# Layer 3 window attention: sums of neighbouring widest states on GpSimd, and one product per stretch of query columns

## The chip, the cores and the metric

The kernel runs on one core of a Trainium2 chip. One launch computes four layers one after the other on an input of 4 images, 256 channels, 48 by 48 pixels, in float32. The metric is the device time of the launch in microseconds (us), as the median of several runs; smaller is better. Five engines work side by side[...]: TensorE (PE in the profile, its weight loads PEld), VectorE (DVE), ScalarE (ACT), GpSimd (POOL) and SyncE (SP), on whose queue nearly all transfers are issued.

## The reference, cut to what matters

Layers 0 to 2 are convolutions and aren't touched. Layer 3 is a windowed linear attention with 8 heads of d = 32 channels, over square windows of 48, 24 and 12 pixels around each pixel:

```python
q = jax.nn.sigmoid(q); k = jax.nn.sigmoid(k)
v = v / jnp.maximum(jnp.linalg.norm(v, axis=1, keepdims=True), 1e-12)
...
for w in WINDOWS:                       # 1, 2, 4
    ws = Hh // w                        # 48, 24, 12
    wk = _box(Ik, ws, Hh, Ww)           # sum of k over the window
    wkv = _box(Ikv, ws, Hh, Ww)         # sum of the 32x32 matrices k v^T over the window
    attn = jnp.einsum('bdhw,bdfhw->bfhw', q, wkv)
    norm = jnp.einsum('bdhw,bdhw->bhw', q, wk)
    attn = attn / (norm[:, None] + 1e-06)
    outs.append(attn.reshape(b, C, Hh, Ww))
```

The three results are concatenated, multiplied by Wout and added to the layer's input. For a pixel, `attn` is the sum over all keys of its window of (q . k) v. It can be computed key by key (scores q . k, masked, times v), or, for a whole tile of keys that a query sees entirely, as q times the tile's state, the 32x32 matrix sum of k v^T.

## The kernel before, in words

**Tiling.** The image is cut into 6 row blocks of 8 rows (`RB`, `NRB`). A key tile is 8 rows by 16 columns, 128 keys (`KC`, and 3 of them side by side, `NKC`). A block of work is one image, one half of the heads (4 heads on 128 partitions) and one row block of queries (384 columns): 4 x 2 x 6 = 48 blocks, in the list `order` (line 2276).

**Steps.** Each block goes through a list of steps (`steps_of`, line 1968). A step computes the scores of some key tiles into PSUM (`scores`, tile `s`), lets ScalarE and VectorE mask them into SBUF (`masked`, tile `sm`; GpSimd masks the smallest window out of the middle one's), and two steps later (`LAG`) multiplies them with the values (`sums`, tiles `acc0` to `acc2`, one per window). The PSUM room for scores is that of one step (`ps_s`, two tiles), so a step's scores can start only when the step before is masked. `whole` (line 2120) is called in step 4 (`WHOLE`) of each block. For the widest window (48, half width 24) it adds what needs no scores: for the key tiles that a query sees entirely, the query times the state. A key tile of column number c is seen entirely by the query columns `cols_whole(c)` (line 100): columns 0 to 24 for c = 0, 8 to 40 for c = 1, 24 to 48 for c = 2. For each of the three c, and each of the four heads, there is one product: 32x32 weights, and 192, 256 or 192 columns (8 rows for each column). A float32 product is two MATMUL instructions in the trace, so a block has 24 of them, all named `acc<-qs,kv`. The four heads lie on four different partition quarters in and out.

**The states.** `window_state(i)` (line 1879) adds on GpSimd the states of the row blocks that are entirely within reach, into the tile `kv` (3 x 32 numbers in each partition): one `tensor_add` for the first two, one for each further row block. It is started at step 3 of the block before (`midway`, line 2316).

**The order of work.** Each engine executes in the order in which this program emits. Beside the steps, jobs written as generators are emitted in between: projections of the next image (`Projection`), the states (`state`), the norms (`norms`, `inverse`), their prefix sums (`k_sums`), and the ends of blocks (`prepare`, `finish`, whose products are `out_ps`). `advance(time, pool_time)` (line 347) is called once a step. `time` is an estimate of what TensorE has to spare in that step (line 2397: 1200 ns + the time of the masks - the time of the sums, where `sums_time`, line 2356, includes `whole`), and goes into a budget, `spare`, that a job's products must find filled (`turn`, `bank`). GpSimd has such a budget too (`slack`): `pool_turn` (line 377) charges `190 + 1.95 * elements` ns for each operation, and an urgent one is charged without waiting.

All instructions go through one helper, so that the profile has line 251 for all; they are told apart by their tiles.

Of the kernel before, what the change touches and what calls it, by code (L numbers as in the profile page):

```python
# [12 lines left out]
F32 = mybir.dt.float32  # L13
# [9 lines left out]
P = 128  # L23
B, C, H, W = 4, 256, 48, 48
# [3 lines left out]
RB = 8  # L28
# [47 lines left out]
HEADS, D = 8, 32  # L76
# [4 lines left out]
NKC = W // KC  # L81
# [18 lines left out]
def cols_whole(c):  # L100

    return max(0, c * KC + KC - HALVES[0]), min(W, c * KC + HALVES[0])


MID = W // 2
# [15 lines left out]
def strips(half):  # L121

    got = []
    for c, x0, x1 in PARTS[half]:
        f0, f1 = cols_whole(c)
        got.append((c, x0, f0) if x0 < f0 else (c, f1, x1))
    return got
# [127 lines left out]
def conv_preact_kernel(  # L255
# [53 lines left out]
    pe, dve, act, pool, sync = (  # L309
        InOrder(tc, e) for e in (nc.tensor, nc.vector, nc.scalar, nc.gpsimd, nc.sync)  # L310
    )
# [57 lines left out]
    def wait_for(*keys):  # L369
        while not made.issuperset(keys):  # L370
            yield 1

    def pool_op(elements):

        return 190 + 1.95 * elements

    def pool_turn(elements, times=1, urgent=False):

        nonlocal slack
        cost = times * pool_op(elements)  # L380
        while slack < 0.5 * cost and not urgent:
            yield 1
        slack -= cost
# [21 lines left out]
    def product_time(columns):  # L405

        return 1.67 * columns
# [192 lines left out]
    with (  # L600
# [479 lines left out]
        def load_row(pool_, tag, a):  # L1080

            t = pool_.tile([P, NCT, K0, P], F32, tag=tag, name="wrow")
            sync.dma_start(
                out=t, in_=w1[:, a * K0 : (a + 1) * K0, :].rearrange("(ct p) k o -> p ct k o", p=P)
            )
            return t
# [442 lines left out]
        with tc.tile_pool(name="wst", bufs=1) as wst:  # L1529
            for ct in range(NCT):  # L1530
                fetch_x(0, ct)
            rows = [load_row(k1p, "k1", 0), load_row(vp, "v", MT), load_row(vp, "v", MT - 1)]
# [15 lines left out]
            for ct in range(NCT):  # L1548
                for k0, k1 in TAPS:
# [3 lines left out]
                    else:  # L1553
                        pool_, tag = {
                            (0, 0): (xp, "x1_0"),
                            (0, 2): (xp, "x1_1"),
                            (1, 0): (wst, "raw1"),
                            (1, 2): (wst, "raw"),
                        }[ct, k0]
# [70 lines left out]
    with (  # L1630
# [248 lines left out]
        def window_state(i):  # L1879


            b, ct, rb = order[i]
            rows = [a for a in range(NRB) if rows_whole(a, rb)]
            yield from wait_for(*(("state", b, ct, a) for a in rows))
            st = states[b, ct]
            yield from pool_turn(NKC * D, len(rows) - 1, urgent=True)
            t = scr.tile([P, NKC, D], F32, tag="kv", name="kv", bufs=2)
            pool.tensor_add(t, st[:, rows[0]], st[:, rows[1]])
            for a in rows[2:]:
                pool.tensor_add(t, t, st[:, a])  # L1890
            wides[i] = t
            made.add(("window", i))

# [16 lines left out]
        def rows_whole(a, rb):  # L1910

            return abs(a - rb) * RB + RB <= HALVES[0]
# [89 lines left out]
        class Block:  # L2002
# [117 lines left out]
            def whole(self, i):  # L2120

                t = wides.pop(i)
                for c in range(NKC):
                    c0, c1 = cols_whole(c)
                    for j in range(HG):
                        head = slice(j * D, (j + 1) * D)
                        pe.matmul(
                            self.accs[0][head].rearrange("p (w r) -> p w r", w=W)[:, c0:c1],
                            t[head, c, :],
                            self.qs[head, c0:c1],  # L2130
                            start=False,
                            stop=False,
                        )
# [182 lines left out]
        def midway(i):  # L2316

            b, ct, rb = order[i]
            if (b, ct) == (0, 0) and 0 < rb <= NRB - seen_first:
                a = seen_first - 1 + rb  # L2320
                until(("k", 0, 0, a), ("v", 0, a))
                load_kv(0, 0, a)
            if ct == NCT - 1:
                start(prepare(i))
            if i + 1 < len(order):
                start(window_state(i + 1), ahead=True)
                nb, nct, nrb = order[i + 1]
                until(("q", nb, nct, nrb))
                qs[i + 1] = load_q(*order[i + 1])
# [18 lines left out]
        def mask_time(st):  # L2348

            on_act = 150 + 0.87 * 2 * (st.hi - st.lo)  # L2350
            if not st.parts[1]:
                return on_act
            on_dve = sum((2 * part[-1] + 130) / 0.96 for part in st.parts[1])
            return 2 * max(on_act, on_dve)

        def sums_time(st, at):

            time = sum(product_time(part[-1]) for parts in st.parts for part in parts)
            if at == WHOLE:
                time += product_time(sum(RB * (c1 - c0) for c0, c1 in map(cols_whole, range(NKC))))  # L2360
            return time

        def far_time(st):
# [2 lines left out]

        blocks, ahead = {}, []
        start(window_state(0))
        start(finish_all())
        for n in range(len(stream) + LAG):  # L2370
            if n < len(stream):
                i, st, at, last = stream[n]
                if at == 0:
                    begun(i)
                ss = blocks[i].scores(st)
                ahead.append(blocks[i].masked(st, ss))
                if at == MIDWAY:
                    midway(i)
            if n >= LAG:
                i, st, at, last = stream[n - LAG]  # L2380
                sms = ahead.pop(0)
                if at == 0:
                    if i >= 2:
                        until(("done", i - 2))
                    blocks[i].begin()
                if at == WHOLE:
                    until(("window", i))
                    blocks[i].whole(i)
                for wi in (1, 0, 2):
                    if st.parts[wi]:  # L2390
                        blocks[i].sums(wi, st, sms)
                if last:
                    done(i)
            time, pool_time = 1000.0, 1000.0
            if LAG <= n < len(stream):
                pool_time = 3600.0 - far_time(stream[n][1])
                time = 1200.0 + mask_time(stream[n][1]) - sums_time(*stream[n - LAG][1:3])
            advance(max(time, 500.0), max(pool_time, 150.0))
# [46 lines left out]
```

## Time and profile before

| | |
|---|---|
| time, median of 3 runs | 3193.77 us (3187.84 to 3198.49) |
| profiled execution: time / span in the profile | 3194.66 us / 3192.8 us |
| PE busy | 2866.5 us, 90% of the span |
| PEld busy | 2024.3 us, 63% |
| DVE busy | 2002.8 us, 63% |
| POOL busy | 1356.8 us, 42% |
| ACT busy | 994.5 us, 31% |
| mean granted TensorE clock | 0.955 |
| first and last product `acc<-qs,kv` of Layer 3 | 1441.3 us, 3169.7 us |
| products `acc<-qs,kv` | 1152 MATMUL |
| additions into `kv` on POOL | 48 of two states, 96 of a further one |

Busy time is that of the whole span. A line of a table of groups names engine, operation and `out<-in` tiles. A window line gives the busy time of each engine within a stretch, with the number of instructions behind it, then the granted TensorE clock, the share in which the transfer engines were busy, and GB/s. A line of the timeline gives the start, the length, the engine and what was executed how many times in a row, and in brackets the idle time before it and what ended that. The chain lists, in order of time, the pieces of work each of which was released by the one before; it leads back from the last instruction, so work that isn't on it was hidden behind something.

### The profile page before, as it was taken

The numbers are of one execution on the slowest core, as the hardware profiler recorded it, in microseconds if no ns is written. First come the engines' busy times: TensorE is split into PE (matmuls) and PEld (weight loads), VectorE is DVE, ScalarE is ACT, GpSimd is POOL, SyncE is SP. The second block draws the span as 40 slices with busy tenths as digits, with TensorE's granted clock in tenths as the row PEclk, the third lists the DMA queues.
The fourth block names the chain that finished last, engine by engine and source line by source line (L and its number), as shares of the span: only waits on it lengthen the run. The fifth ranks groups of instructions, "written<-read, shape, count | busy, mean of one in ns | idle before, by whom it ended". The sixth has DMA issues, their size and how long they took to land.

```text
span 3192.8 us, 98649 instructions
## 1 busy us (share of the span) xinstructions
PE 2866.5 (90%) x42698; PEld 2024.3 (63%) x42698; DVE 2002.8 (63%) x3779; ACT 994.5 (31%) x1965; POOL 1356.8 (42%) x1915
## 2 busy tenths in 40 slices
PE   3678999898989987889998899898999989999999
PEld 2456868677766856576665556565666655666665
DVE  7976658747855831376776666675546765555454
ACT  0002211121111144325543235553236532333322
POOL 0000012003000312046788877787757687644443
PEclk9788899999999988899999999999999999999999
DMA  8746512431443144324565765564544456411222
GB/s 276 212 161 185 159 62 103 130 123 53 136 123 110 60 127 146 111 79 140 162 200 147 215 187 156 163 192 142 162 138 144 141 157 186 134 40 44 89 76 69
DMA packets 380037, 434.05 MB, mean 136 GB/s; under 512 B 129843, under 2 KB 335443, under 8 KB 378451
## 3 DMA queue, kind: packets, MB, share of 16 engines
q1 hardware_dynamic: 378403, 425.76, 43.3%
q8 instruction: 338, 5.54, 0.8%
q0 software_dynamic: 144, 1.17, 0.2%
q10 hardware_dynamic: 1056, 0.79, 0.1%
q14 instruction: 96, 0.79, 0.1%
HBM read 288.11 MB, written 140.68 MB: 134 GB/s over the span
## 4 chain that ended last, share of the span: by engine, by line
PE 62%; DVE 11%; POOL 4%; DMA 4%; ACT 3%; issue 2%; SPq 2%; ACTq 0%; DVEq 0%; POOLq 0%
PE s L251 16%; PE cv L251 15%; PE acc L251 15%; PE out_ps L251 5%; PE proj_ps L251 5%; PE ap L251 3%; DVE sm L251 2%; DVE l2v L251 2%; SPq L251 2%; POOL sm L251 2%; POOL nhi L251 1%; ACT sm L251 1%; DVE v L251 1%; PE keys_ps L251 1%; DVE x L251 1%
## 5 line engine op out<-in xcount | busy, mean ns | idle before, releaser
L251 DVE TENSOR_TENSOR sm<-s,masks 128x448 f32<-128x448 f32 (+9 forms) x1408 | 619.9, 497 | 437.1 <-PE s L251 379.5
L251 POOL TENSOR_TENSOR sm<-sm,masks 128x704 f32<-128x704 f32 (+11 forms) x512 | 596.5, 1186 | 513.9 <-DVE sm L251 513.5
L251 ACT ACTIVATE sm<-s 128x384 f32<-128x384 f32 (+2 forms) x736 | 441.5, 609 | 746.6 <-PE s L251 589.7
L251 PE MATMUL cv<-vx,wt 128*128 128x288 f32 x2080 | 562.6, 427 | 92.2 <-DVE vx L251 49.9
L251 PE MATMUL s<-qs,ks 32*128 32x320 f32 (+10 forms) x8704 | 589.1, 360 | 34.7 <-ACT sm L251 20.1
L251 PE MATMUL acc<-sm,vs 128*32 128x128 f32 (+19 forms) x18432 | 606.0, 276 | 6.3 <-issue 6.2
L251 PEld LDWEIGHTS acc<-sm,vs 128*32 128x32 f32 x18432 | 443.0, 110 | 190.2 <-issue 143.4
L251 PEld LDWEIGHTS s<-qs,ks 32*128 32x128 f32 x8704 | 395.1, 186 | 256.2 <-issue 112.0
L251 PEld LDWEIGHTS cv<-vx,wt 128*128 128x128 f32 x2080 | 404.5, 199 | 214.6 <-issue 56.8
L251 POOL MEMSET v<- 128x16 f32 (+1 forms) x120 | 18.7, 216 | 765.0 <-DVE vx L251 639.8
L251 PE MATMUL cv<-v,wl 128*128 128x384 f32 x1152 | 226.8, 357 | 27.3 <-DVE x L251 9.4
L251 PEld LDWEIGHTS cv<-v,wl 128*128 128x128 f32 x1152 | 216.7, 197 | 38.4 <-issue 17.9
L251 DVE TENSOR_SCALAR sm<-s 128x896 f32<-128x896 f32 (+1 forms) x96 | 110.9, 1156 | 116.0 <-PE s L251 92.5
L251 PE MATMUL s<-masks 24*128 24x192 bf16 (+3 forms) x1664 | 168.3, 284 | 0.0
L251 POOL TENSOR_TENSOR v<-l2v,v 128x384 fp32r<-128x384 f32 x96 | 108.5, 1160 | 120.4 <-ACT v L251 111.7
L251 PE MATMUL cv<-pad,wl 128*128 128x384 bf16 x864 | 145.5, 331 | 5.1 <-ACT pad L251 5.1
L251 POOL TENSOR_TENSOR nhi<-nhi,nq 128x384 f32<-128x384 f32 x144 | 147.9, 1047 | 0.0
L251 PE MATMUL out_ps<-o,wout_sb 128*32 128x384 f32 x1152 | 122.0, 495 | 6.2 <-ACT ns L251 2.4
L251 PEld LDWEIGHTS <-wl 128*128 128x128 bf16 x864 | 84.5, 98 | 65.5 <-issue 7.9
L251 PE MATMUL out_ps<-stage,wout_sb 128*32 128x384 f32 x1152 | 121.8, 491 | 0.2 <-issue 0.2
L251 DVE TENSOR_TENSOR pt<-cs 128x184 f32<-128x184 f32 x144 | 120.1, 838 | 0.1
L251 PE MATMUL ap<-seen,xT 120*128 120x120 f32 (+3 forms) x832 | 120.1, 304 | 0.0
(175 smaller groups left out, 3419.8 us busy)
## 6 DMA issues: line engine op xcount, KB each, us to landing
wt<-wt SPq DMA_DIRECT2D x48, 768.0 KB
kb_d<-pt SPq DMA_DIRECT2D x48, 576.0 KB
rc<-r_d SPq DMA_DIRECT2D x192, 144.0 KB
nhi<-kb_d SPq DMA_DIRECT2D x120, 192.0 KB
nlo<-kb_d SPq DMA_DIRECT2D x88, 192.0 KB
o_d<-stage SPq DMA_DIRECT2D x24, 576.0 KB
o<-o_d SPq DMA_DIRECT2D x24, 576.0 KB
wl<-wl_d SPq DMA_DIRECT2D x16, 768.0 KB
```

The source lines that it names most:

```text
L251: return lambda *args, **kwargs: self.tc.keep_in_program_order(op(*args, **kwargs))
```

## The change

The query columns are cut where the set of entirely seen key tiles changes: at 0, 8, 24, 40 and 48. Columns 0 to 8 see tile 0 alone, 8 to 24 tiles 0 and 1, 24 to 40 tiles 1 and 2, 40 to 48 tile 2 alone. GpSimd makes two more states for each block, 0 + 1 and 1 + 2, with one further `tensor_add` of 64 numbers in each partition, and `whole` then runs one product for each head and stretch: 64, 128, 128 and 64 columns. The tile `kv` grows from 3 x 32 to 5 x 32 numbers. The two estimates that the planner uses, of the cost on GpSimd and of the columns in `whole`, follow.

```diff
+def whole_ranges():
+
+    cuts = sorted({x for c in range(NKC) for x in cols_whole(c)})
+    got = []
+    for x0, x1 in zip(cuts, cuts[1:]):
+        cs = [c for c in range(NKC) if cols_whole(c)[0] <= x0 and x1 <= cols_whole(c)[1]]
+        got.append((x0, x1, cs))
+    return got
+
+
+WHOLES = whole_ranges()
...
-            yield from pool_turn(NKC * D, len(rows) - 1, urgent=True)
-            t = scr.tile([P, NKC, D], F32, tag="kv", name="kv", bufs=2)
-            pool.tensor_add(t, st[:, rows[0]], st[:, rows[1]])
+            yield from pool_turn(NKC * D, len(rows), urgent=True)
+            t = scr.tile([P, 2 * NKC - 1, D], F32, tag="kv", name="kv", bufs=2)
+            alone, pairs = t[:, 0:NKC], t[:, NKC:]
+            pool.tensor_add(alone, st[:, rows[0]], st[:, rows[1]])
             for a in rows[2:]:
-                pool.tensor_add(t, t, st[:, a])
+                pool.tensor_add(alone, alone, st[:, a])
+            pool.tensor_add(pairs, alone[:, 0 : NKC - 1], alone[:, 1:NKC])
...
-                for c in range(NKC):
-                    c0, c1 = cols_whole(c)
+                for x0, x1, cs in WHOLES:
                     for j in range(HG):
                         head = slice(j * D, (j + 1) * D)
                         pe.matmul(
-                            self.accs[0][head].rearrange("p (w r) -> p w r", w=W)[:, c0:c1],
-                            t[head, c, :],
-                            self.qs[head, c0:c1],
+                            self.accs[0][head].rearrange("p (w r) -> p w r", w=W)[:, x0:x1],
+                            t[head, cs[0] + (NKC if len(cs) == 2 else 0), :],
+                            self.qs[head, x0:x1],
...
-                time += product_time(sum(RB * (c1 - c0) for c0, c1 in map(cols_whole, range(NKC))))
+                time += product_time(sum(RB * (x1 - x0) for x0, x1, _ in WHOLES))
```

More of the change, by code (lines that the diff above doesn't have):

```diff
@@ L102, in cols_whole @@
     return max(0, c * KC + KC - HALVES[0]), min(W, c * KC + HALVES[0])
+def whole_ranges():
[6 more added lines that the diff above has]
+WHOLES = whole_ranges()
+assert all(cs in ([c] for c in range(NKC)) or cs in ([c, c + 1] for c in range(NKC - 1)) for _, _, cs in WHOLES)
 MID = W // 2
```

## The prediction

> **What bounds the kernel now.** I read the page's busy times first, then the windows by stage, the timeline around one widest product, the chain of waits in each 50 us of Layer 3, and the waits. Busy times of PE and POOL over the whole span, then four windows (length, then PE, PEld, DVE, ACT, POOL busy, clock, DMA share):
>
> ```profile
> PE 2866.5 (90%) x42698; PEld 2024.3 (63%) x42698; DVE 2002.8 (63%) x3779; ACT 994.5 (31%) x1965; POOL 1356.8 (42%) x1915
> ...
> 1693.00:1772.00 79.00, 58.94 (x1024) 33.76 (x1016) 44.63 (x80) 21.16 (x50) 70.39 (x91) 0.87 0.57 165
> 2012.00:2032.00 20.00, 11.82 (x328) 8.98 (x320) 10.76 (x21) 3.99 (x13) 15.14 (x27) 0.88 0.79 202
> 2032.00:2215.00 183.00, 180.62 (x4007) 117.85 (x4008) 137.18 (x242) 89.77 (x194) 151.84 (x224) 0.98 0.50 157
> 2690.00:3193.00 503.00, 478.91 (x10616) 320.94 (x10608) 258.38 (x511) 152.88 (x275) 235.52 (x248) 0.99 0.28 80
> ```
>
> The reader is to see that Layer 3 has two regimes. In most of it (2032 to 2215 stands for it) PE is busy 95 to 99%: time taken off PE there is time taken off the run. In short stretches around the norms of an image (1693 to 1772: PE 75%, POOL 89%) something else leads. The chain says what:
>
> ```profile
> 1734.52 2.51 POOL sm L251 x2
> 1737.03 1.43 POOL nhi L251
> 1738.46 2.50 POOL sm L251 x2
> 1740.96 1.43 POOL nhi L251
> ```
>
> There POOL works without a pause and PE waits for the norm's operands. Four stretches are led by POOL, the SP queue or a transfer: 1693-1772, 1861-1885, 2012-2032 and 2560-2690. (One at 2215-2230 has no widest product in it.)
>
> The widest product itself, in the timeline of one block:
>
> ```profile
> 2326.83 1.28 PE L251 MATMUL acc<-qs,kv 32*32 32x192 f32 x24
> 2328.05 0.66 PE L251 MATMUL acc<-sm,vs 128*32 128x156 f32 x16
> ```
>
> From its start to the next group's it takes 2328.05 - 2326.83 = 1.22 us. And a block in which the masks lead, not PE:
>
> ```profile
> 2864.66 2.40 DVE L251 TENSOR_TENSOR sm<-s,masks 128x312 f32<-128x312 f32 x8 [1.23 <-PE s L251]
> 2864.67 1.28 PE L251 MATMUL acc<-qs,kv 32*32 32x192 f32 x24
> 2865.89 1.05 PE L251 MATMUL acc<-sm,vs 128*32 128x112 f32 x32
> 2866.87 1.27 PE L251 MATMUL s<-qs,ks 32*128 32x320 f32 x13
> ```
>
> DVE reads the scores until 2867.06; the next scores begin at 2866.87 in the half already read and need the other half at once. A shorter widest product would only make PE wait here.
>
> **What the skill says.** (1) "TensorE: Matmul & The Clock Gate", Part 3, The mechanism: matmuls at different 32x32 tile positions run concurrently, their starts some 4 ns apart. The trace agrees: 24 instructions of 192 or 256 columns in 1.22 us are possible only with four heads at once. (2) The same page, Back-to-back issue gap: for 1 to 64 columns there is an issue floor of about 60 cycles, 25 ns. The 64-column stretches of the change lie at it, so it is my upper bound for them; the trace speaks against it as a price per instruction of a group of four (`kv_ps` below: 8 ns each). (3) "TensorEngine Tiling (Array Packing)", Key Properties: changing the tiling mode drains the engine. The mode changes into and out of the widest product remain, so that cost stays. (4) "GPSIMD Engine Reference", 3.1: a two-input float32 add costs about 2.6 cycles an element, over a fixed dispatch; the trace agrees (next part).
>
> **The change part by part.**
>
> *Products on PE.* Prices of four concurrent heads, one instruction each ("a quad"), come from the chain:
>
> ```profile
> 2302.44 0.19 PE kv_ps L251 x24
> ...
> 2319.24 0.66 PE keys_ps L251 x24
> ...
> 2331.65 1.29 PE out_ps L251 x16
> ```
>
> Six quads of 32 columns take 0.19 us, 32 ns each; six of 128 columns 0.66 us, 110 ns; four of 384 columns 1.29 us, 322 ns. From 128 columns up that is 0.84 to 0.86 ns a column. Before: four quads of 192 (161 ns) and two of 256 (215 ns) = 1.07 us, so that 0.15 of the 1.22 us is fixed. After: four quads of 128 = 0.44 us and four of 64. I take 56 ns for these (the same line, 0.86 to 0.88 ns a column): 0.22 us. Sum 0.66 + 0.15 = 0.81 us; 0.41 us saved in a block, 48 x 0.41 = 19.7 us. Bounds for the 64-column quad: not under 32 ns, since 32 columns take that; not over 4 x 25 = 100 ns, the page's issue floor paid four times (an estimate). That gives 0.51 to 0.23 us a block, 24 to 11 us in all. The 8 further weight loads are 32x32, 105 ns each and overlapped; 24 of a larger form pass within 0.19 us in `kv_ps`, so no cost.
>
> *The addition on POOL.* 128x64 isn't in the trace; its neighbours are:
>
> ```profile
> L251 POOL TENSOR_TENSOR kp<-kp,carry x5: 282/288/387, 1705.5 to 1770.3; 128x48 f32<-128x48 f32 x5
> ...
> L251 POOL TENSOR_TENSOR kv<-kv,state x96: 386/390/876, 1440.5 to 3126.9; 128x96 f32<-128x96 f32 x96
> ```
>
> 48 numbers take 288 ns, 96 take 390: 2.1 ns each, so 64 take 0.32 us (bounds 0.29 and 0.39). 48 x 0.32 = 15.4 us of POOL. Queued behind it are masks for the smallest window and norm work. Away from the stretches POOL idles for DVE (487.0 us in the list of waits), which hides it. The state is made a block ahead; PE waited for `kv` once in the run, 1.8 us, in the first block. There the addition lies bare: 0.3 us, about cancelled by the first group's running at a lower clock, where the saving is larger.
>
> *Saving that isn't kept.* Six widest products start in stretches led by others (1714.8, 1868.2, 2015.5, 2571.0, 2601.6, 2650.3): 6 x 0.41 = 2.5 us lost. Five of these are on POOL's side and pay the addition as well: 5 x 0.32 = 1.6 us. In two more the masks end with the product as in the timeline above (1789.7, 2899.0) and nothing covers: 0.7 us. Some eight have 0.36 to 0.40 us between masks and scores: 8 x 0.05 = 0.4 us. Together 5.2 us. In two others of that pattern (2191.3, and 2864.7, the one shown) the emitted order of the changed kernel has `out_ps` products (1.29 us) put into the step, which cover the wait; were they not, 0.8 us more would be lost.
>
> *What is moved.* The planner finds 0.43 us more to spare in step 4 of every block and charges GpSimd 0.38 us more. In the emitted order of the two kernels the projections come about one step earlier (888 of 1092 instructions), out products too, and the norms of the last image up to some six steps later. No instruction kind changes in number, but for 6 divisions that go straight from PSUM on DVE and save 6 copies on ACT. The transfers issued by SP are the same 1710, in slightly other places. Cost: nothing on average, for the sum of inserted PE work is the same; but which of the waits at the norms get longer or shorter isn't fixed, and single ones are 2.7 to 8.3 us long. I carry +-8 us for it.
>
> *Sum.* 3194.66 (the profiled execution, of which 1.9 lie outside the span) - 19.7 + 5.2 = 3180.2. That execution was 0.9 above the median of 3193.77, so 3179.3 for a median; I say 3180. What is late next is what is now: PE, and in the stretches POOL.
>
> **The rivals.**
>
> *A. The forecast*, a net gain of 7 to 22 us, 3180.
>
> *B. The waits at the norms shrink as well.* PE idles at the norms for about 20 + 8 + 9 + 13 us in the stretches. With norms emitted later against PE, some of the waits fall away. For: of the 144 norm products 39 move later and 12 earlier. Against: their POOL work moves with them. Full 19.7 and 6 us of waits: 3168.
>
> *C. The time doesn't go.* POOL's 15.4 us would lie on the path in most blocks, since POOL is 83% busy in 2032-2215, and PE would wait for masks in place of its own products. For: mask waits follow every block. Against: in that stretch PE is 99% busy, with POOL waiting for DVE. About 3191.
>
> *D. Slower: a store of V stuck behind norm loads on SP.*
>
> ```profile
> ACT vt L251 <- DMA v_d<-vt: 13.2, 2, 10.4
> ```
>
> At 2021-2031 ACT waits 10.4 us for the store of an earlier `vt`, which SP issues only after a row of norm loads; PE then idles 8.3 us in front of `proj_ps`. With projections a step earlier, more stores could fall into such rows. To be slower by 0.3% it needs 14 + 9.6 = 24 us, three more such stalls: 3180 + 25 = 3205. Against it: in the emitted order, stores of `vt` with ten or more norm loads among the 22 transfers before them are 6 before and 5 after.
>
> **How the numbers follow.** A 0.58, B 0.14, C 0.18, D 0.10. 0.3% is about what a measurement of this kernel can tell from no change: 9.6 us, so faster is under 3184.2, slower over 3203.4. Of A some 0.06 lies above 3184.2. Faster 0.52 + 0.14 = 0.66; within 0.06 + 0.18 = 0.24; slower 0.10. The range of 3166 to 3196 takes in A, most of B and two thirds of C, and with them both ends of the 64-column price (3175 to 3189).
>
> **What would show it.** In the profile after: the widest product at 0.8 us from start to next group (right), near 1.0 if the issue floor holds (PE's step wrong); `kv<-kv` 128x64 at 0.32 us; PE busy lower by some 20 us with its idle time in Layer 3 up by a few; POOL up by 15 us; waits of PE and PEld for POOL `nhi` within some us of their 64. The forecast is wrong if these waits, or that for `v_d<-vt`, grow by 10 us or more, or shrink so.

## The result, and the profile after

The change takes 3166.98 us (median of 8 runs, 3147.29 to 3175.78) against 3193.52 us before (8 runs beside it): a ratio of 0.9912, 95% interval 0.989 to 0.9933. By that ratio it is 28 us less (the two medians themselves lie 26.5 us apart; from here on, differences between run times are taken from the ratios). Two repeats on other occasions gave 0.9919 (0.9906 to 0.9931) and 0.9924 (0.9908 to 0.994), or 26 and 24 us. Forecast were 14.

The profiled execution took 3175.78 us, its span 3174.0. Busy times on its page:

```profile
PE 2852.3 (90%) x43082; PEld 2034.6 (64%) x43082; DVE 1989.3 (63%) x3779; ACT 991.4 (31%) x1959; POOL 1368.6 (43%) x1963
```

POOL has 48 more instructions and 11.8 us more work; PE is 14 us less busy. From the first widest product on, PE is busy 1661.7 us before and 1639.7 us in the change, which is 22 us less; the rest of the difference lies in Layers 0 to 2. One widest product in the timeline of the change, the counterpart of the one at 2326.83 before:

```profile
2326.01 0.86 PE L265 MATMUL acc<-qs,kv 32*32 32x64 f32 x32
...
2326.80 0.66 PE L265 MATMUL acc<-sm,vs 128*32 128x156 f32 x16
```

From its start to the next group's: 0.79 us, where it was 1.22. GpSimd's additions into `kv`, from the groups of that tile (minimum/median/maximum ns):

```profile
L265 POOL TENSOR_TENSOR kv<-kv,state x96: 384/388/746, 1445.6 to 3107.9; 128x96 f32<-128x96 f32 x96
L265 POOL TENSOR_TENSOR kv<-state x48: 377/388/874, 1445.1 to 3107.5; 128x96 f32<-128x96 f32 x48
L265 POOL TENSOR_TENSOR kv<-kv x48: 317/320/892, 1446.4 to 3108.4; 128x64 f32<-128x64 f32 x48
```

The added one has a median of 320 ns. The block led by masks, which the forecast showed at 2864.66, now:

```profile
2848.05 2.40 DVE L265 TENSOR_TENSOR sm<-s,masks 128x312 f32<-128x312 f32 x8 [1.23 <-PE s L265]
2848.06 0.86 PE L265 MATMUL acc<-qs,kv 32*32 32x64 f32 x32
...
2848.86 1.05 PE L265 MATMUL acc<-sm,vs 128*32 128x112 f32 x32
2849.84 1.56 PE L265 MATMUL s<-qs,ks 32*128 32x320 f32 x12
```

The scores begin 0.61 us before DVE is done with the scores of the step before (2850.45), 0.42 us earlier in that pass than they did, and no `out_ps` product stands between. From this widest product to that of the next block it takes 34.23 us, and 34.22 before: the saving is lost here. The chain of waits around the first norms of an image, the counterpart of 1734.52:

```profile
1735.51 2.39 POOL sm L265 x2
...
1738.02 1.36 POOL nhi L265
1739.38 2.50 POOL sm L265 x2
1741.89 1.43 POOL nhi L265
```

That stretch is still led by POOL. The waits that the forecast named:

```profile
PEld norm_ps L265 <- POOL nhi L265: 39.2, 21, 8.5
...
PE norm_ps L265 <- POOL nhi L265: 16.8, 7, 7.8
```

For the norms' input the two queues of TensorE wait 56.0 us together (one wait often counts in both). Before:

```profile
PEld norm_ps L251 <- POOL nhi L251: 46.7, 29, 7.1
...
PE norm_ps L251 <- POOL nhi L251: 17.5, 8, 6.4
```

That is 64.2 us.

In what follows, "Layer 3" is the time from the first product `acc<-qs,kv` to TensorE's last instruction, and "interval i" that from block i's widest product to block i + 1's (blocks count from 0). Layer 3 took 1747.3 us before and 1723.5 in the change. Layers 0 to 2 are emitted alike in all kernels here, yet in the profiles the first widest product starts anywhere between 1425.7 and 1446.4 us, so spans are compared in Layer 3. Even that spreads: three profiles of the change have 1723.5, 1724.1 and 1717.6.

### The profile page after: what moved, and what is told of

Read it like the earlier page. It is cut to its first block, busy times and chain, and to the rows that moved or that the text cites. A ratio compares the mean times of both kernels' runs of the same rounds, so it can differ in the third digit from the quotient of the medians.

```text
span 3174.0 us, 99454 instructions
## 1 busy us (share of the span) xinstructions
PE 2852.3 (90%) x43082; PEld 2034.6 (64%) x43082; DVE 1989.3 (63%) x3779; ACT 991.4 (31%) x1959; POOL 1368.6 (43%) x1963
## 4 chain that ended last, share of the span: by engine, by line
PE 63%; DVE 11%; ACT 3%; POOL 3%; DMA 3%; issue 3%; SPq 1%; ACTq 0%; DVEq 0%; POOLq 0%
PE s L265 17%; PE cv L265 15%; PE acc L265 15%; PE out_ps L265 6%; PE proj_ps L265 5%; PE ap L265 3%; DVE sm L265 2%; DVE l2v L265 2%; ACT sm L265 1%; DVE v L265 1%; POOL sm L265 1%; PE keys_ps L265 1%; SPq L265 1%; DVE x L265 1%; DVE k L265 1%
## 5 line engine op out<-in xcount | busy, mean ns | idle before, releaser
L265 POOL MEMSET v<- 128x16 f32 (+1 forms) x120 | 18.6, 214 | 765.2 <-DVE vx L265 639.0
L265 PE MATMUL cv<-v,wl 128*128 128x384 f32 x1152 | 227.2, 358 | 25.8 <-DVE x L265 8.2
```

Of the source, the lines that this page charges most:

```text
L265: return lambda *args, **kwargs: self.tc.keep_in_program_order(op(*args, **kwargs))
```

## The experiments

### Products, order and addition by themselves

**products_only.** The change with the planner's two figures of before, so that all other work is emitted in the order of before.

```diff
-            yield from pool_turn(NKC * D, len(rows), urgent=True)
+            yield from pool_turn(NKC * D, len(rows) - 1, urgent=True)
-                time += product_time(sum(RB * (x1 - x0) for x0, x1, _ in WHOLES))
+                time += product_time(sum(RB * (c1 - c0) for c0, c1 in map(cols_whole, range(NKC))))
```

> The changed products and the additional sum on GpSimd, but the planner's two figures as before, so that every other instruction is emitted in the order of before. Theory (the products gave what was forecast, the emitted order the rest): 13 to 16 us below before. Rival (the products gave it all, because a shorter group also shortens waits behind it): 24 to 30 us below before. Rival (the order gave it all, the freed time of TensorE is lost in waits): within 5 us of before.

**order_only.** The kernel before, products and states unaltered, with the two figures of the change: its order without its products.

```diff
-            yield from pool_turn(NKC * D, len(rows) - 1, urgent=True)
+            yield from pool_turn(NKC * D, len(rows), urgent=True)
-                time += product_time(sum(RB * (c1 - c0) for c0, c1 in map(cols_whole, range(NKC))))
+                time += product_time(RB * W)
```

> The products of before and no additional sum, but the planner's two figures of the change, so that every instruction is emitted in the order of the change. Theory: the waits at the norms of the last image go, 10 to 14 us below before. Rival (products gave it all): within 4 us of before. Rival (order gave it all): 24 to 30 us below before.

**sum_only.** The kernel before, with the two pair sums made on GpSimd and read by nobody.

```diff
-            t = scr.tile([P, NKC, D], F32, tag="kv", name="kv", bufs=2)
-            pool.tensor_add(t, st[:, rows[0]], st[:, rows[1]])
+            t = scr.tile([P, 2 * NKC - 1, D], F32, tag="kv", name="kv", bufs=2)
+            alone, pairs = t[:, 0:NKC], t[:, NKC:]
+            pool.tensor_add(alone, st[:, rows[0]], st[:, rows[1]])
...
+            pool.tensor_add(pairs, alone[:, 0 : NKC - 1], alone[:, 1:NKC])
```

> Before, with the additional sum on GpSimd made in each block and read by nobody; products and order as before. By the forecast 1 to 3 us slower than before, for GpSimd leads in few stretches only; if GpSimd's 15 us lay on the path, 10 us slower or more; if the norm waits depend on GpSimd by chance, anything of either sign up to 5 us.

**change_again.** The change, beside these three.

> The changed kernel once more, for a second profile: its times so far spread from 3147 to 3176 us, before's only from 3188 to 3198. Theory: about 3167 as median, and in the profile the norms of the last image without long waits of TensorE; if the spread has a place, the two profiles of this kernel differ in it.

| run | median, us | ratio to before (95%) | us against before | Layer 3, us |
|---|---|---|---|---|
| before | 3189.13 | | | 1747.3 |
| products_only | 3169.51 | 0.9943 (0.9923 to 0.9963) | -18.2 | 1727.5 |
| order_only | 3177.27 | 0.9958 (0.9946 to 0.997) | -13.4 | 1733.7 |
| sum_only | 3188.85 | 0.9998 (0.9985 to 1.0011) | -0.6 | 1744.7 |
| change_again | 3165.82 | 0.9919 (0.9906 to 0.9931) | -25.8 | 1724.1 |

The products give what was forecast or a little more (products_only lies between its theory and its first rival), the addition costs nothing that shows, and the order, which was priced at nothing, gives 13 us (9.6 to 17.2), as order_only's theory had it. The widest product in the timeline of products_only is as short as in the change:

```profile
2301.64 0.86 PE L265 MATMUL acc<-qs,kv 32*32 32x64 f32 x32
2302.43 0.66 PE L265 MATMUL acc<-sm,vs 128*32 128x156 f32 x16
```

### Where the order's gain is

By intervals, order_only differs from before mainly in two: 31 (-11.4 us) and 32 (-6.4); the change there has -10.8 and -6.7, products_only +0.5 and -0.1. Some 3 and 5 us come back in 33 and 35. The timeline of before within interval 31:

```profile
2620.26 0.85 PE L251 MATMUL norm_ps<-nhi,head_sel 128*32 128x384 f32 x6
...
2624.57 3.70 PE L251 MATMUL norm_ps<-nhi,head_sel 128*32 128x384 f32 x6 [3.46 <-POOL nhi L251]
...
2628.83 0.85 PE L251 MATMUL out_ps<-o,wout_sb 128*32 128x384 f32 x8 [0.56 <-ACT ns L251]
```

The two halves of a norm (a 0.85 us piece each) stand directly behind one another, and `out_ps` behind them: from the first to the `out_ps` it takes 8.57 us for 1.7 us of products. The second half waits for `nhi`, which POOL had not made yet. The same norm in the change:

```profile
2623.24 0.85 PE L265 MATMUL norm_ps<-nhi,head_sel 128*32 128x384 f32 x6 [0.23 <-DVE res L265]
...
2626.66 0.82 PE L265 MATMUL norm_ps<-nhi,head_sel 128*32 128x384 f32 x6
```

Between the halves stand 2.6 us of a step's own products, and nothing waits for POOL.

### Four runs on the norms' place

The first theory was that what counts is how far apart, or how late, the norms are emitted. **norms_spaced** holds two norms of the last image back by five steps, in before; **products_norms_spaced** does so in products_only:

```diff
+            if b == B - 1 and rb in (2, 3):
+                yield 5
```

> Before, with one edit: the third and the fourth norm of the last image are held back by 5 steps each, so that they and those after them are emitted about where the change has them; products, sum and everything else as before. Theory (the order's gain is the wait at these norms): 9 to 13 us below before, in the blocks 30 to 36. Rival (the gain of the emitted order comes from projections and out products moved earlier everywhere): within 3 us of before.

> The products and the sum of the change, the planner's figures of before, and the same two norms held back. Theory (both parts add up): 27 to 31 us below before, a little under the change itself. Rival (they share a gain): about 18 us below before, as the products alone.

**sums_figure_only** takes from the change the figure for the sums alone, without that for GpSimd:

```diff
-                time += product_time(sum(RB * (c1 - c0) for c0, c1 in map(cols_whole, range(NKC))))
+                time += product_time(RB * W)
```

> Before with only one of the two planner figures changed, that of the columns in the widest product; the emitted order then moves in the first three images, but leaves the norms of the last image where before has them. Theory: within 5 us of before. Rival (more time to spare for TensorE's jobs is what helps): 9 to 14 us below before, as with both figures.

**change_norms_later** lets two steps more pass, in the change, between a norm's work on GpSimd and its products:

```diff
-            yield 1
+            yield 3
```

> The change with every norm's product two steps further behind its work on GpSimd, in all images. If TensorE's waits at the norms of the first two images (some 13 us in the profile of the change between 1745 and 1775) go too: 8 to 13 us below the change. If the norms are only late then, because blocks wait for them at their end: slower than the change.

Measured, against 3188.70 before: norms_spaced 3193.82, ratio 1.0014 (1.0001 to 1.0028); products_norms_spaced 3175.64, 0.9955 (0.9938 to 0.9972), which is products_only without a further gain; sums_figure_only 3185.92, 0.9993 (0.9981 to 1.0005); change_norms_later 3182.65, 0.9982 (0.9968 to 0.9995), slower than the change by some 20 us. The theory fell: room between a norm and its products is no gain in itself. With the figure for the sums alone nothing is gained, as expected, so the figure for GpSimd is needed, which points at GpSimd's share of planned time; that figure by itself wasn't run.

### Four runs on GpSimd's steps for V

In order_only GpSimd normalises the last tile of V between 2554 and 2582 us; in before it does so in pieces between 2568 and 2604, so that the last of it lies in interval 31, which starts at 2601.6. The second theory was that this placement is the cause. **last_v_early** makes these steps urgent in before, **products_last_v_early** in products_only, **change_two_v_early** does it in the change for the last tiles of images 1 and 3, counted from 0 (there the condition is `b in (1, 3)`):

```diff
-                yield from pool_turn(n, 4)
+                yield from pool_turn(n, 4, urgent=b == B - 1 and a == NRB - 1)
...
-                yield from pool_turn(C)
+                yield from pool_turn(C, urgent=b == B - 1 and a == NRB - 1)
```

> Before, with one edit: GpSimd's normalisation of the last V tile of the last image (16 small operations and 3 of 256 numbers) is emitted without waiting for GpSimd's budget, 4 to 5 steps earlier; products, additional sum and planner figures as before. In the profiles so far the four kernels with this work early (the change twice, the order alone, the norms later) are 11 us shorter in the interval of block 31, the five with it late are not. Theory (this work in front of the second norm of the last image is what TensorE waited for): 8 to 13 us below before, 9 to 12 of them in block 31. Rival (the gain of the order is spread over other moves): within 4 us of before.

> The products and the sum of the change, the planner's figures of before, and the last V tile of the last image normalised early as in last_v_early. Theory (two separate gains add up): 18 us from the products and 8 from the early V tile, 24 to 28 us below before, as the change itself. Rival (they share a gain): 16 to 20 us below before.

> The change, with the normalisation of the last V tile emitted without waiting for GpSimd's budget in the second and the last image. It moves the norms of the first image's end apart and those of the second to earlier steps, the last image's as in last_v_early. If waits of TensorE at the norms of block 8 (some 27 us with their low clock in the profile of the change) shrink: 5 to 12 us below the change. If not, within 4 us of the change.

**change_last_v_late** delays them in the change, which brings the last image's norms back to where before has them:

```diff
-            yield 1
+            yield 4 if b == B - 1 and a == NRB - 1 else 1
```

> The change, with one edit: the same normalisation is held back by three more steps, to where before has it; the norms of the last image then stand where before has them too, all else is as in the change. Theory: the change loses 8 to 13 us, in blocks 30 to 36, and is 14 to 18 us below before. Rival: within 4 us of the change.

Measured: last_v_early 3181.83 against 3191.93, 0.9976 (0.9963 to 0.9989), or 7.7 us less (3.5 to 11.8), but without the gain in interval 31 that its theory asked for; products_last_v_early 3174.61 against 3186.97, 0.9957 (0.9942 to 0.9972), or 13.7 us less, no better than products_only and short of both its theory and its rival. change_two_v_early 3194.89 against 3186.97, 1.0025 (1.0013 to 1.0037): slower than before, which neither of its expectations allowed for. change_last_v_late alone did as expected: 3172.65 against 3191.93, 0.9951 (0.9934 to 0.9967), so that some 9 to 12 us of the change's gain are gone, and the wait is back in its timeline:

```profile
2614.79 0.85 PE L265 MATMUL norm_ps<-nhi,head_sel 128*32 128x384 f32 x6
2618.86 0.83 PE L265 MATMUL norm_ps<-nhi,head_sel 128*32 128x384 f32 x2 [3.22 <-POOL nhi L265]
...
2622.52 0.85 PE L265 MATMUL out_ps<-o,wout_sb 128*32 128x384 f32 x8 [0.61 <-POOL o L265]
```

So the place is right, and the V steps have to do with it, but making them early in before isn't enough. Something stands between them and the wait.

### The flush at a block's start

Line 2384 holds a block back until the one two before it is done, because there are two `stage` tiles:

```python
if i >= 2:
    until(("done", i - 2))
```

`until` calls `advance()` with an unlimited budget until that holds. All waiting jobs then emit what they have at once: a flush. Counting its rounds in the program's own emission, at the start of block 32:

| kernel | rounds at block 32 | gain in interval 31 |
|---|---|---|
| before, products_only, sum_only, sums_figure_only, norms_spaced, products_norms_spaced, change_last_v_late | 7 | no |
| last_v_early, products_last_v_early, change_two_v_early | 5 | no |
| change, order_only, change_norms_later | 1 | yes |

The other flushes of more than two rounds are the same size in before and the change (11 rounds at block 9, 5 at 12, 6 at block 20 or 21, 5 at 24). In place of the 11 at block 9, change_norms_later has new ones (9 at block 20, 5 at 36), and so has change_two_v_early (12 at 10, 9 at 12). So the count at block 32 tells who has the gain there; it doesn't rank whole runs. The seven rounds come about because the output of block 30, which GpSimd has to multiply first (`prepare`), doesn't fit into GpSimd's planned share in time. With the V steps late again it doesn't in the change either (change_last_v_late); with these steps alone made early five rounds are left (last_v_early). **block30_early** takes just this link, in before; **products_block30_early** in products_only:

```diff
-                yield from pool_turn(NB)
+                yield from pool_turn(NB, urgent=i == 30)
                 pool.tensor_mul(o[:, wi], o[:, wi], rcs[0][:, wi])
```

> The kernel before; only the three multiplications by which GpSimd prepares the output of block 30 no longer wait for their share of GpSimd's planned time. So block 30 is emitted as done before block 32 begins, and the seven rounds that were emitted at once at that point (both halves of a norm, then block 30's output products) are gone; six such rounds appear at the start of block 36 instead of one. Theory (the order's gain is the flush that goes): intervals of blocks 31 and 32 shorter by 12 to 18 us together, without the 6 us wait for the norm's input; some 3 to 8 us given back around block 36; in all 5 to 12 us below before. Rival (the order gains because of where GpSimd's own steps stand, as in the run with the last V early): within 5 us of before, and the loss ahead of the norm stays.

> The change's products at the order of before, and the same edit for block 30. Theory: the two gains add, 23 to 30 us below before (18 from the products, 5 to 12 from the flush). Rival (the products and the order draw on the same idle time): 16 to 20 us below before.

**change_all_early** makes that step, and the multiplications for the norms by which GpSimd finishes `nhi` (the expectations call them additions), urgent everywhere, in the change; **last_image_no_flush** makes them so for the last image's norms and blocks 30, 33 and 34, in before (conditions `b == 3` and `i in (30, 33, 34)` in place of `True`):

```diff
-                    yield from pool_turn(NB)
+                    yield from pool_turn(NB, urgent=True)
...
-                yield from pool_turn(NB)
+                yield from pool_turn(NB, urgent=True)
```

> The change; GpSimd's steps that prepare the outputs and its additions for the norms are emitted without waiting for their share of planned time, for every block. Of the five flushes of more than two rounds at block starts (11, 5, 6, 5 and some of two) only one of seven is left. Theory (a flush costs TensorE about 1 us a round): 8 to 20 us below the change, 36 to 48 below before. Rival (GpSimd gets these steps ahead of the masks and sums that TensorE needs sooner, and the wait only moves): within 5 us of the change, or slower than it.

> The kernel before; GpSimd's preparation of the outputs of blocks 30, 33 and 34, and its additions for the last image's norms, no longer wait for their share of planned time. No block from 32 to 37 then starts with a flush of more than two rounds. Theory: the 15 us that block30_early gave back in the interval of block 35 stay away, and blocks 30 to 37 are together 10 to 20 us shorter than before; Layer 3 is so too, and the run 9 to 20 us below before. Rival (the idle time is set by the amount of GpSimd's work in this stretch, not by the flush): blocks 30 to 37 no more than 8 us shorter, as in block30_early, with the loss at another block.

**change_third** and **change_all_early_again** are repeats, on one chip.

> The change itself, unaltered, beside last_image_no_flush and change_all_early_again on one chip: 25 to 30 us below before.

> change_all_early once more, beside the change: 8 to 18 us below the change, 36 to 46 below before, with Layer 3 within 2 us of the 1706.7 us of its first profile.

| run | median, us | before | ratio (95%) | us against before | Layer 3, us |
|---|---|---|---|---|---|
| block30_early | 3183.71 | 3186.11 | 0.9994 (0.9977 to 1.001) | -1.9 | 1739.7 |
| products_block30_early | 3166.02 | 3186.11 | 0.9932 (0.9909 to 0.9955) | -21.7 | 1722.8 |
| last_image_no_flush | 3179.53 | 3188.77 | 0.9966 (0.9952 to 0.9979) | -10.8 | 1735.8 |
| change_third | 3162.59 | 3188.77 | 0.9924 (0.9908 to 0.994) | -24.2 | 1717.6 |
| change_all_early | 3148.02 | 3186.11 | 0.9872 (0.9847 to 0.9897) | -40.8 | 1706.7 |
| change_all_early_again | 3142.89 | 3188.77 | 0.9863 (0.9844 to 0.9882) | -43.7 | 1705.4 |

Intervals 31 and 32 together, in the windows of four kernels (length; busy time of PE, PEld, DVE, ACT, POOL, each with its instructions; clock; DMA share; GB/s). Before:

```profile
2601.63:2695.36 93.73, 85.41 (x1684) 51.13 (x1688) 52.26 (x92) 27.13 (x54) 73.62 (x79) 0.98 0.56 169
```

products_only, with the flush:

```profile
2573.17:2667.37 94.20, 85.06 (x1708) 51.45 (x1699) 52.57 (x92) 27.01 (x54) 73.53 (x80) 0.98 0.54 163
```

block30_early, without it:

```profile
2604.57:2679.72 75.15, 72.37 (x1616) 47.33 (x1615) 47.39 (x89) 25.30 (x49) 59.84 (x69) 1.00 0.51 158
```

The change, without it:

```profile
2598.31:2674.60 76.29, 74.63 (x1688) 48.78 (x1686) 50.37 (x92) 25.73 (x50) 59.91 (x65) 1.00 0.58 172
```

94 us with the flush, 75 to 76 without, whatever the products. One edit of one step of one block reproduces the order's effect at its place (-18.6 us, and -17.8 in order_only). It does so partly by moving work: PE has 68 instructions fewer in there than before (32 at `out_ps`, 24 at `kv_ps`, 12 at `norm_ps`, some 4 us by what such groups take elsewhere, an estimate), and POOL has 65 to 69, and had 79. That is why the whole run gains less. block30_early gives 15.1 us back in interval 35, where its new flush stands ahead of block 36:

```profile
2773.59 0.93 PE L251 MATMUL norm_ps<-nhi,head_sel 128*32 128x384 f32 x6 [0.83 <-DVE res L251]
...
2777.13 3.39 PE L251 MATMUL norm_ps<-nhi,head_sel 128*32 128x384 f32 x6 [2.61 <-POOL nhi L251]
```

The pattern is that of before at 2620: the halves back to back, the second waiting for POOL. last_image_no_flush has no such flush, and interval 35 is only 3.8 us above before; but 33 and 30 are 3.8 and 2.6 above, and it ends up in the same place. For intervals 30 to 36 as a whole, the windows of before and of block30_early are

```profile
2571.06:2833.79 262.73, 246.67 (x5184) 155.62 (x5188) 148.36 (x271) 78.58 (x154) 180.26 (x202) 0.99 0.48 139
2572.28:2827.10 254.82, 239.04 (x5184) 151.78 (x5183) 145.65 (x271) 77.81 (x152) 180.76 (x202) 0.98 0.50 144
```

PE has the same 5184 instructions in both, so no work of PE has left this stretch, and it is 7.9 us shorter. The saving shows as busy time of PE and not as idle time, 4.7 us of it at `norm_ps` (17.29 against 12.55 in these windows): in before, the half at 2624.57 gets its operands one by one and counts as busy for 3.70 us, the half at 2620.26 for 0.85. The same stretch takes 254.5 us in last_image_no_flush and 252.0 in order_only. Over all kernels here it takes 257.8 to 271.6 us with seven rounds at block 32, 258.2 to 269.0 with five, and 247.2 to 254.8 with one or none.

So the expectation of last_image_no_flush held for the run (-10.8) but not for the stretch (-8.2, where 10 to 20 were expected). The times of the two runs with the edit for block 30 don't confirm the 8 us: block30_early, at -1.9 us (-7.3 to +3.2), missed its 5 to 12, while its Layer 3 was 7.6 us shorter; products_block30_early, at -21.7 (-29.0 to -14.3), lies between its theory and its rival and doesn't tell them apart, while its stretch is 254.6 us and that of products_only 261.2.

What follows: by the profiles, this flush cost about 8 us net, 8 of the 10.7 us by which order_only shortens this stretch. A flush has no fixed price by the round, as the theory had it. The second flush, ahead of block 36, cost nothing that shows between these two kernels (254.8 with it, 254.5 without), although GpSimd is behind there as well; yet norms_spaced, which has seven rounds at block 32 and six at block 36, takes 271.6 us for the stretch, 8.9 more than before. And change_norms_later has one round instead of 11 ahead of block 9, with interval 8 29.6 us shorter than before, but gives it back in the next ones: its blocks 6 to 13 take 322.6 us, those of the change 322.7. What sets the price of a flush isn't shown.

change_all_early is the test elsewhere. Blocks 6 to 13, then 14 to 25, in the windows of the change:

```profile
1655.23:1977.95 322.72, 294.63 (x6195) 181.32 (x6191) 204.28 (x364) 114.85 (x242) 253.62 (x294) 0.96 0.62 181
1977.95:2430.26 452.31, 429.36 (x9575) 276.00 (x9571) 279.60 (x520) 197.70 (x399) 334.05 (x461) 0.99 0.52 156
```

And of change_all_early:

```profile
1644.48:1933.81 289.33, 277.71 (x6183) 178.78 (x6181) 198.28 (x354) 111.91 (x235) 218.69 (x265) 0.99 0.59 171
1933.81:2400.81 467.00, 433.61 (x9561) 277.68 (x9557) 283.55 (x524) 192.60 (x390) 364.11 (x488) 0.97 0.56 168
```

With nearly the same TensorE instructions the first stretch is 33.4 us shorter, where the flush of 11 rounds stood ahead of block 9; 14.7 come back in the second, where POOL has 30 us more to do; Layer 3 as a whole is 16.8 us shorter. On one chip it is 19.7 us faster than the change (3142.89 and 3162.59). TensorE's waits for the norms' input, from 56.0 us:

```profile
PEld norm_ps L265 <- POOL nhi L265: 19.8, 15, 9.5
...
PE norm_ps L265 <- POOL nhi L265: 10.8, 4, 9.4
```

30.6 us. This version beats both kernels. Whether the gain is in the flushes or in the earlier multiplications for the norms can't be told from it, since the edit does both; that change_norms_later gained nothing over these blocks without the flush of 11 rounds speaks for the multiplications, without showing it.

## Why the prediction was right in sign and wrong in size

- **The products**: right. 0.81 us for a group was forecast and 0.79 measured, 1.22 - 0.79 = 0.43 us in a block and some 20 us in all (19.7 forecast). Between the forecast's two prices for the 64-column product the trace decides: the issue floor of 25 ns for up to 64 columns ("TensorE: Matmul & The Clock Gate", Back-to-back issue gap) isn't paid four times by four concurrent heads; their quads start 55 to 56 ns apart in the trace, close to the 56 that I took from a straight line.
- **The addition**: right. 0.32 us forecast, 0.320 measured, and hidden, as far as the run can tell: sum_only is at -0.6 us (-4.8 to +3.5).
- **Saving that isn't kept**: 5.2 us forecast; the mechanism is seen at two places, the size isn't settled. products_only ran 18.2 us (11.8 to 24.6) below before and its Layer 3 was 19.8 us shorter, so by that profile hardly anything of the 20 was given back in all. The six intervals in stretches led by others together kept nothing (+0.2 us, where 2.5 would have been saved), but singly they go from -1.1 (the one at 1868.2) to +1.6 us. Of the two led by masks, the one at 2899.0 kept nothing; the one at 1789.7 is 0.9 us shorter, but so it is in sum_only, which has the old products. The one at 2864.7, for which I had counted on `out_ps` as cover, kept nothing either: the lines shown have none. Other intervals gained more than 0.42 us (1.6 in interval 3, 1.8 in 21, 3.2 in 41); these single amounts weren't tested.
- **What is moved**: the step that failed. It was priced at nothing on average, with +-8 us, on the argument that the inserted TensorE work sums to the same. order_only measured -13.4 us (-17.2 to -9.6). The argument leaves out that the same work can cost more where it is emitted in a heap: the same 5184 instructions keep PE busy 246.67 us in the order of before and 239.04 in block30_early. With the new figures, GpSimd's steps for the last V tile and the preparation of block 30's output are emitted earlier; the flush ahead of block 32 shrank from seven rounds to one, and with it went the wait of TensorE for `nhi` at that place. Undoing it in the change costs some 9 to 12 us (change_last_v_late); doing away with the flush alone in before shortens intervals 31 and 32 by 18.6 us and the stretch by 7.9 by the profile (block30_early), which its run time doesn't confirm. The sign that the forecast had named for this, waits for `nhi` that shrink by 10 us or more, stayed silent: in sum they shrank by 8.2. At the last image's norms (2580 to 2700 us) they went from 14.1 to nothing, but at the first image's (1700 to 1800 us) they grew from 25.8 to 33.7.
- **The rivals**: B was nearest ("the waits at the norms shrink as well"), with 6 us for them and the full 19.7; its 3168 is about the measured time. That is in part luck, for its reason was off: norms emitted later were no gain (norms_spaced, change_norms_later). C fell with sum_only and products_only. D didn't happen: the waits of ACT for the store of V, in the list of waits of the change,

```profile
ACT vt L265 <- DMA v_d<-vt: 6.6, 1, 6.6
```

  are 6.6 us, and were 13.2.

**What stays open.** Products and order by themselves sum to 31.6 us; the change has 24 to 28. The intervals of the runs cover the difference, so that it may be nothing. Layer 3 in the profiles points to a loss that the two share (19.8 and 13.6 us shorter by themselves, and 23.8, 23.2 and 29.7 in three profiles of the change), without showing it. Of the order's 13 us, 8 are tied, by the profiles, to the flush ahead of block 32; the rest is spread over Layer 3, partly as work moved between neighbours (interval 19 is 15.9 us longer in order_only, 20 is 19.0 shorter), and no run isolates it.

## What to carry to other kernels

When a program emits its engines' order from cost estimates, an edit of an estimate is an edit of the schedule: give the order a price of its own, by running the old work in the new order and the new work in the old one. Look for places where such a planner must catch up, and emits in a heap what it had put off: there an in-order engine meets operands that another engine hasn't made yet. Such a place cost 8 us here and another nothing that shows, so each has to be tried by itself, and a change should be followed over several blocks, since part of what one interval gains is work that moved to another.

## What was not expected of the hardware

- A wait can stand in the busy time of a profile: six products of a norm count 0.85 us where their operands are ready (before, 2620.26), and 3.70 us where GpSimd makes the operands while they run (2624.57).
- Layers 0 to 2, with the same instructions in the same order, ended 20.7 us apart in the profiles (1425.7 to 1446.4). In three profiles of the change they ended at 1446.4, 1437.2 and 1438.5 us, with spans of 3174.0, 3165.5 and 3160.4, so a good part of the spread of the whole run's time can be theirs; the cause wasn't sought.
- Two things came as forecast. Eight more weight loads in a block, a third more, cost nothing that shows (PEld for `acc<-qs,kv` 0.70 us within 0.79). And POOL's 64-number addition lies within 2 ns of the line of its neighbours: 288, 320 and 388 ns for 48, 64 and 96 numbers in a partition.
